# Staging fresh silus in the halves of the edge tile, inner residues first, and other places for the statistics' work and the silu stores

## The chip, the cores and the metric

One core of a Trainium2 chip runs the whole program. Its engines are TensorE (PE, with its weight loads as PEld), VectorE (DVE), ScalarE (ACT), GpSimd (POOL) and SyncE (SP), which here only issues DMA transfers, one after another in the program's order. The metric is the device time of one execution in microseconds (us); the time before is the median of three runs.

## The reference

The input is `x` of 4 x 128 x 96 x 96 in float32. A group norm (32 groups) is followed by a scan block that runs over four readings of each image (columns and rows, each forward and reversed), and the four results are fused by a 1x1 convolution and added to `x`. The block, for one reading:

```python
t = _grouped1x1(x, in_proj_w, in_proj_b, G)
u, gate = (t[:, :HID], t[:, HID:])
u = jax.nn.silu(u)
u = conv over 5 neighbours along the sequence, depthwise
s = _conv1x1(u, ssm_in_w)
a = DMIN + (DMAX - DMIN) * sigmoid(_conv1x1(u, ssm_delta_w, ssm_delta_b))
bb, cc = tanh(_conv1x1(u, ssm_b_w, ssm_b_b)), tanh(_conv1x1(u, ssm_c_w, ssm_c_b))
prefix = jnp.cumsum(jnp.log(a), axis=-1)
hst = jnp.exp(prefix) * jnp.cumsum(bb * s * jnp.exp(-prefix), axis=-1)
u = u + _conv1x1(cc * hst + ssm_d * s, ssm_out_w)
u = _grouped1x1(u * sigmoid(gate), mix_w, mix_b, G)
return _conv1x1(u, out_proj_w, out_proj_b)
```

There are 256 hidden channels and 32 states. The kernel folds the norm into the projection's weights, and the last two convolutions and the fusion into one matrix (`w_fin`).

## The kernel before

**Pairs, steps, phases.** A sequence of 9216 places is cut into 6 stretches of 16 image lines and 4 residues (place modulo 4), 384 places each. One *pair* handles one residue of one stretch for the forward and the reversed reading together. Four pairs, in the order of residues 1, 2, 3, 0, are a *step*; six steps are a *phase* (columns or rows of one image); eight phases, a column and a row phase for each of the four images (batches), make 48 steps and 192 pairs, numbered t = 0 to 191. So batches 2, 3 and 4 begin at steps 12, 24 and 36, that is with pairs 48, 96 and 144.

**Fresh and mirrored steps.** The reversed reading meets the same places from the other end. Therefore only the first three steps of a phase (the *fresh* ones) compute the projection and its Silu; the other three read them backwards: the fourth and fifth still have the tiles of the third and second, and the sixth loads what the first step stored. The gates (tanh halves of sigmoid) of the first half are kept in DRAM in the same way and loaded back (`load_kept`) two pairs before they are used, into two tiles that alternate.

**Fronts.** A front (`new_front`, `new_silu`, `new_stage`, `new_rest`) makes one residue of a later step: four matmuls, three Silus on ACT, and the moves. Channels 128 to 255 go straight to their plane of the step's `sil` tile. Channels 0 to 127 must lie in another order of partitions (32 channels times 4 residues), so ACT writes them to a *stage*, and four DMAs of 98.6 kB move it to `sil` (L525). There are two stages, cut from the tile `shared`; front g uses stage g modulo 2, so it has to wait until the moves of the front two before have landed. In pair t the front of residue index t + 5 is made, five pairs ahead of its step's first pair. During the warm-up (pairs 0 to 5) whole fronts are made five pairs ahead by simpler code, and the tenth is made in pair 6 in two halves that share two banks.

**The lone edge.** For residues 0 and 3 the five taps reach into a neighbouring column of which one residue alone is needed, in the plain order of channels. DVE adds it (`add_lone`, L766) from the tile `lone`, which holds the silus of residues 0 and 3 in stage order: 4 slots, two for residue 0 and two for residue 3. For that, each fresh step stores the two stages of residues 0 and 3 to DRAM (`edge`, or `front` for the first step), and `load_lone` (L757) loads both, 770 KB, at each step's first pair, except where the fourth step reuses the third's.

**One pair** (`pair_on`). PE: convolution into banks 6 and 7 (L130 on `band` and `less`), the output products of an older pair (L130 on `w_fin`), the z products (L649) mixed with a gate's or a front's matmuls (L629, L491), then the projection to the states (L130 `psum<-u,main`). DVE: four taps (L819), the edge (L766) in pairs of residues 3 and 0 (*short* pairs, whose convolution needs no `less`), a scan in the first two pairs of a step (L894), the gating of the pair six before (L710). ACT: copies, tanhs, the first tap of the next pair (L817), behind the gating, and then the front's stage (L518), which reads the banks that the next convolution writes. POOL: decay, products of the scan, and the additions into the accumulator. The order of all engines is written out by hand; nothing is rescheduled.

**Statistics.** While a column phase runs, the next image is loaded in 24 chunks (`xs`, L429), two for each short pair, and `bn_stats` (L437) runs on each. The rest (`stats_finish`: `bn_aggr`, small products, a square root by Newton steps on POOL, scaled weights, their rolled copy by DMA) is spread over pairs of the row phase by a table of places (pair within the phase, point in the pair).

**The start of a phase** also stores the first step's silus (`keep_silu`, L565, two stores of 770 KB), and in the column phases of later batches finished lines go out (L913) and new image lines come in (L1059).

## Time and profile before

| | us |
|---|---|
| median of three runs (lowest, highest) | 1758.65 (1758.1, 1760.34) |
| the profiled execution | 1758.79 |
| its span, from first to last instruction | 1757.0 |
| PE busy | 1713.8 |
| DVE busy | 1508.5 |
| ACT busy | 1484.5 |
| POOL busy | 1470.6 |
| step 1 (pairs 4 to 7, warm-up) | 36.27 |
| step 44, pairs 176 to 179 | 34.75 |
| step 12 (first of batch 2) | 42.80 |

A line of the profile names the source line, the engine, the operation and the tiles (out<-in), then how often and how long, and behind the bar or in brackets the idle time before it with what ended it. A wait that names ACT or DVE may be the end of a chain that a late DMA began. Matmul ends are modelled and overlap. The 16 DMA engines moved 386.30 MB, 220 GB/s over the span, but unevenly: between 123 and 307 GB/s in fortieths of the span. Rows of stretches give for each engine the busy time and, in brackets, the instructions; their ends were chosen at the starts of projections, so that a stretch is one step.

### The profile page before, as it was taken

Reading aid. Unit: us, or ns where it says so; the run is one execution under the profiler, and the core shown is the slowest. Engines: PE = TensorE matmul, PEld = TensorE weight load, DVE = VectorE, ACT = ScalarE, POOL = GpSimd, SP = SyncE. Lnnn points to the kernel's source line nnn. Section 1 sums busy time; section 2 is a strip of 40 time slices with the busy share of each in tenths; the row PEclk is TensorE's granted clock in tenths of the full one; section 3 lists DMA queues with packets and bytes.
Section 4 is the critical chain, followed back from the end, with each engine's and each line's share of the span. In section 5 each row is a group of like instructions: output and inputs, shape, how many; then the busy total and the mean of one; then the engine's idle time right before and its main releaser. Section 6 shows DMA issues by size and latency. Waiting matters only on the chain.

```text
span 1757.0 us, 50266 instructions
## 1 busy us (share of the span) xinstructions
PE 1713.8 (98%) x20410; PEld 705.5 (40%) x20410; DVE 1508.5 (86%) x1508; ACT 1484.5 (84%) x2438; POOL 1470.6 (84%) x1452
## 2 busy tenths in 40 slices
PE   7999999999999999999989999999999999999998
PEld 3343344344343434444434434444344443444333
DVE  6899999888789998888878999888887888888897
ACT  4788888888788888888968888888887888888875
POOL 3589898988678989888867898988787889998887
PEclk9999999999999999999999999999999999999999
DMA  7755896468995788547899487843899638873475
GB/s 240 224 181 181 268 260 194 139 208 243 296 307 187 227 245 242 176 134 253 246 294 296 147 251 240 250 155 133 246 276 298 232 123 273 238 212 131 134 238 175
DMA packets 149382, 386.30 MB, mean 220 GB/s; under 512 B 19873, under 2 KB 86305, under 8 KB 149153
## 3 DMA queue, kind: packets, MB, share of 16 engines
q1 hardware_dynamic: 149008, 383.05, 70.5%
q8 instruction: 162, 2.65, 0.6%
q14 instruction: 68, 0.55, 0.1%
q10 hardware_dynamic: 144, 0.04, 0.0%
HBM read 215.12 MB, written 133.01 MB: 198 GB/s over the span
## 4 chain that ended last, share of the span: by engine, by line
PE 86%; DMA 5%; DVE 2%; ACT 2%; POOL 2%; issue 1%; SPq 0%; ACTq 0%; POOLq 0%; DVEq 0%
PE psum L130 70%; PE psum L649 6%; PE psum L629 5%; PE psum L491 4%; DMA gate<-kept 2%; DMA kept<-shared 1%; DMA out<-acc 1%; ACT shared L518 1%; DVE t L894 1%; DMA sil<-shared 1%; DVE u L710 1%; DVE psum L819 1%; DMA acc<-in_xr 1%; POOL t L900 0%; POOL t L868 0%
## 5 line engine op out<-in xcount | busy, mean ns | idle before, releaser
L819 DVE SCALAR_TENSOR_TENSOR psum<-sil,small,psum 128x768 f32<-128x768 f32 x576 | 589.1, 1023 | 51.5 <-ACT psum L817 32.4
L130 PE MATMUL psum<-u,w_fin 128*32 128x384 f32 (+1 forms) x6192 | 558.9, 488 | 1.1 <-ACT ys L935 0.4
L130 PE MATMUL psum<-u,main 128*32 128x384 f32 x6144 | 535.6, 489 | 1.6 <-DVE u L1003 1.1
L710 DVE SCALAR_TENSOR_TENSOR u<-gate,psum 128x768 f32<-128x768 f32 x376 | 341.8, 950 | 150.9 <-PE psum L649 66.2
L954 POOL TENSOR_TENSOR acc<-ys,acc 128x384 f32<-128x384 f32 x375 | 442.0, 1202 | 12.5 <-ACT ys L935 1.9
L130 PEld LDWEIGHTS psum<-u,w_fin 128*32 128x32 f32 x6192 | 204.9, 110 | 310.3 <-issue 209.6
L661 ACT COPY psum<-u 128x768 f32<-128x768 f32 x384 | 306.8, 799 | 6.8 <-DVE u L710 4.0
L130 PEld LDWEIGHTS psum<-u,main 128*32 128x32 f32 x6144 | 180.1, 110 | 327.9 <-issue 207.0
L900 POOL TENSOR_TENSOR t<-t,t 64x384 f32<-64x384 f32 (+1 forms) x192 | 262.8, 1369 | 57.1 <-DVE t L894 37.4
L130 PE MATMUL psum<-sil,band 128*32 128x384 f32 x3072 | 290.1, 489 | 19.6 <-ACT shared L518 18.0
L867 POOL TENSOR_SCALAR t<-tm 64x384 f32<-64x384 f32 x188 | 179.6, 956 | 134.6 <-ACT tm L856 122.5
L649 PE MATMUL psum<-t,main 32*128 32x384 f32 x1536 | 272.8, 520 | 3.0 <-ACT psum L661 2.3
L901 POOL TENSOR_TENSOR t<-t,t 64x384 f32<-64x384 f32 (+1 forms) x192 | 236.9, 1234 | 15.1
L868 POOL TENSOR_TENSOR t<-t,tm 64x384 f32<-64x384 f32 x192 | 227.0, 1182 | 25.4 <-ACT t L859 10.3
L817 ACT ACTIVATE psum<-sil,small 128x768 f32<-128x768 f32 x191 | 172.0, 901 | 35.4 <-DVE u L710 31.5
L819 DVE SCALAR_TENSOR_TENSOR u<-sil,small,psum 128x768 f32<-128x768 f32 x192 | 194.9, 1015 | 6.8
L937 ACT COPY ys<-psum 128x384 f32<-128x384 f32 x288 | 138.4, 481 | 53.1 <-PE psum L130 42.6
L130 PEld LDWEIGHTS psum<-sil,band 128*32 128x32 f32 x3072 | 106.7, 109 | 170.8 <-issue 71.4
L629 PE MATMUL psum<-x_in,wn 32*128 32x384 f32 x768 | 162.4, 497 | 0.0
L491 PE MATMUL psum<-x_in,wn 32*128 32x385 f32 x704 | 149.7, 503 | 1.7 <-ACT shared L518 1.0
L503 ACT ACTIVATE sil<-psum,bnorm 128x385 f32<-128x385 f32 x176 | 102.4, 583 | 48.3 <-PE psum L491 35.4
L665 ACT ACTIVATE gate<-psum,bnorm 128x384 f32<-128x384 f32 x168 | 97.4, 582 | 43.4 <-PE psum L629 26.7
(110 smaller groups left out, 1701.0 us busy)
## 6 DMA issues: line engine op xcount, KB each, us to landing
gate<-kept SPq DMA_DIRECT2D x106, 768.0 KB, 5.7
kept<-gate SPq DMA_DIRECT2D x82, 768.0 KB, 3.8
sil<-shared SPq DMA_DIRECT2D x352, 96.2 KB, 3.5
sil<-sil SPq DMA_DIRECT2D x32, 770.0 KB, 8.2
lone<-edge SPq DMA_DIRECT2D x26, 770.0 KB, 8.6
x_in<-in_xs SPq DMA_DIRECT2D x194, 96.2 KB, 3.3
out<-acc SPq DMA_DIRECT2D x46, 384.0 KB, 7.5
x_in<-in_xs SPq DMA_DIRECT2D x88, 192.5 KB, 5.3
```

The source lines that it names most:

```text
L130: nc.tensor.matmul(o[r, : rhs.shape[-1]], lhsT, rhs, start=start, stop=stop, skip_group_check=True)
L491: nc.tensor.matmul(bank(banks[2 * j + s])[:, : N + 1], stats[units[step * UB]["b"]][0][a, s, :], x_in[s][a, q, :], start=True, stop=True,)
L629: nc.tensor.matmul(bank(to)[:, :N], stats[un["b"]][0][r, s, :], x_in[s][r, q, off : off + N], start=True, stop=True)
L649: nc.tensor.matmul(bank(ssm(bi, s) + j)[:, :N], w_so[r, bass.ts(j, P)], z[r, :], start=(bi, s) not in seeded, stop=True, skip_group_check= ...
L661: nc.scalar.copy(psum[:, ssm(bi, s) : ssm(bi, s) + 2, :N], us[bi][:, s])
L710: nc.vector.scalar_tensor_tensor(v, g, 1.0, pz, ALU.add, ALU.mult)
L819: nc.vector.scalar_tensor_tensor(us[i][:, :, 1, :] if k == K - 1 else part, src, w_tap[:, k : k + 1], part, ALU.mult, ALU.add,)
L867: nc.gpsimd.tensor_scalar(*decay(i))
L868: nc.gpsimd.tensor_mul(ta[0:64, p, :], tb[0:64, :], tm[0:64, :])
L900: engine.tensor_mul(ta[0:64, p, r], tb[64:P, r], ta[64:P, p, r])
L901: engine.tensor_add(tb[0:64, r], ta[0:64, p, r], tb[0:64, r])
L954: adder.tensor_add(part, y, part)
```

## The change

It does the following.

- Fronts take the residues in the order 1, 2, 0, 3 (`PLANES`) instead of 0, 1, 2, 3. The two loads of projection inputs per step take the planes 1 and 2, then 0 and 3 (`SETS`), and the saved planes of the first step are split in the same way: planes 1 and 2 are contiguous, 0 and 3 are not.
- A front's stage is a half of the step's own `lone` tile: front f uses half f modulo 2. After the fourth front the tile holds residues 0 and 3, in the order in which `add_lone` reads them. So fresh steps from step 2 on have no load of `lone`: 22 loads less. First and third steps of a phase use `shared` for it, second steps the tile that mirrored steps load into.
- Only second steps store edges to DRAM (and first steps their `front`); third steps no longer do.
- The two stores of a first step's silus are issued one pair earlier.
- Chunks of statistics begin in the phase's second step in batches 2 and 3, as they do in the first batch, and end in the next phase's first step. `stats_finish` keeps its operations, each two to five pairs later.
- In the warm-up, front 10 is made in pair 5 behind front 9.
- In pairs 55, 103 and 151 the decay runs on POOL again instead of ACT.

The core of the diff:

```diff
+PLANES = (1, 2, 0, 3)
+    SETS = (slice(1, 3), slice(0, R, 3))
...
-            (0, 0): gather,
-            (1, 1): means,
...
-            (3, 0): guess,
...
-            (8, 2): roll,
+            (6, 0): gather,
+            (7, 1): means,
...
+            (10, 0): guess,
...
+            (14, 2): roll,
...
-        places = singles * 2
-        if ph == 0:
-            places = (singles[2:] + [NP + 2, NP + 3]) * 2
+        places = (singles[2:] + [ph * NP + NP + 2, ph * NP + NP + 3]) * 2
...
+    def stage_of(step, f):
+        return lone[step][:, 2 * (f % 2) : 2 * (f % 2) + 2, :]
...
+        if st == 0:
+            nc.sync.dma_start(kept_front[e][PLANES[f]], stage)
+            if f == R - 1:
+                keep_silu(step, 0)
+        elif st == 1:
+            if f > 1:
+                nc.sync.dma_start(edge_of(step)[f - 2], stage)
+            if f == 0 and step > 1:
+                keep_silu(step - 1, 1)
...
+    def lone_tile(step):
+        if step % NS in (0, 2) and step > 1:
+            t = shared()[:, : 4 * (N + 1)]
+        else:
+            t = wk.tile([P, 4 * (N + 1)], F32, tag="lone", bufs=1, name=f"lone_{step}")
+        return t.rearrange("p (a n) -> p a n", n=N + 1)
...
-        by_scalar = i == NU - 2 or i > 2 * NP and i // 2 % (2 * NP) == 7
+        by_scalar = i == NU - 2
...
-            else:
-                whole_front(t + R, (4, 5, 2, 3) if banks != PROJ else (6, 7, 2, 3))
+            for f in {4: (8,), 5: (9, 10)}.get(t, ()):
+                whole_front(f, (4, 5, 2, 3) if banks != PROJ else (6, 7, 2, 3))
...
-        elif k == 0:
+        elif k == 0 and un["st"] > NS // 2:
             load_lone(un["step"])
...
-            later.update({(a + R, at): f for (a, at), f in stats_finish(un["b"] + 1).items()})
+            later.update(stats_finish(un["b"] + 1))
```

How it moves instructions, at three places. First, the queue of SP from the last front of step 12 on (pairs 46 to 48). `sil_202` is the saved silus in DRAM, `front_204` and `edge_1` are stored stages, `acc` and `out` are image lines in and out, `xs` chunks, `gate_` the tiles of kept gates. Before:

```order
L534 DMA front_204<-shared 128x770
L1059 DMA acc<-in_xr 128x2x384 x2
L913 DMA out<-acc 128x2x384 x2
L429 DMA xs_0_4665<-in_xr 128x384
L429 DMA xs_1_4667<-in_xr 128x384
L525 DMA sil_4690<-shared 32x770 x4
L686 DMA gate_177<-kept_6_196 128x1536
L536 DMA edge_1_207<-shared 128x770
L565 DMA sil_202<-sil_4305 128x1540
L757 DMA lone_4738<-front_204 128x2x770
L429 DMA xs_2_4758<-in_xr 128x384
L525 DMA sil_4690<-shared 32x770 x4
```

and next `L686 DMA gate_176<-kept_1_191`; the second store to `sil_202` comes behind that gate. Now, up to the same gate:

```order
L532 DMA front_204<-shared 128x770
L566 DMA sil_202<-sil_4295 128x1540
L1068 DMA acc<-in_xr 128x2x384 x2
L922 DMA out<-acc 128x2x384 x2
L523 DMA sil_4677<-lone_4678 32x770 x4
L687 DMA gate_177<-kept_6_196 128x1536
L566 DMA sil_202<-sil_4295 256x1x770
L523 DMA sil_4677<-lone_4678 32x770 x4
L687 DMA gate_176<-kept_1_191 128x1536
```

Both stores of saved silus stand ahead of the second gate; chunks, edge store and edge load are gone from this stretch.

Second, ACT in pairs 5 and 6 of the warm-up (L503 or L505 the Silus into `sil`, L518 or L516 the stage, L661 or L662 the copies ahead of the z products). Before:

```order
L503 ACTIVATE sil_743<-psum,bnorm_268 128x385 x2
L518 ACTIVATE shared<-psum,bnorm_268 128x770
L856 ACTIVATE tm_1_2_0_842<-psum,small 128x384
L859 COPY t_0_1_2_0_825<-psum 64x384
L865 ACTIVATE t_0_1_2_0_825<-psum,small 64x384
L661 COPY psum<-u_0_1_0_378 128x2x384
L503 ACTIVATE sil_743<-psum,bnorm_268 128x385 x2
L518 ACTIVATE shared<-psum,bnorm_268 128x770
L661 COPY psum<-u_0_1_0_378 128x2x384
```

Now:

```order
L505 ACTIVATE sil_743<-psum,bnorm_268 128x385 x2
L516 ACTIVATE shared<-psum,bnorm_268 128x770
L505 ACTIVATE sil_743<-psum,bnorm_268 128x385 x2
L516 ACTIVATE shared<-psum,bnorm_268 128x770
L865 ACTIVATE tm_1_2_0_852<-psum,small 128x384
L868 COPY t_0_1_2_0_835<-psum 64x384
L874 ACTIVATE t_0_1_2_0_835<-psum,small 64x384
L662 COPY psum<-u_0_1_0_378 128x2x384 x2
```

The tenth front's three Silus moved from between the two copies of pair 6 to ahead of pair 5's own tanhs.

Third, DVE in step 7, where `bn_aggr` (L236 or L237) ends the sums of batch 2 (L894 is the scan, L766 or L775 the edge). Before:

```order
L819 SCALAR_TENSOR_TENSOR u_1_1_0_2894<-sil_2460,small,psum 128x2x384
L894 SCALAR_TENSOR_TENSOR t_6_2594<-t_6_2594 64x768
L236 BN_AGGR mv_2474<-bn_868 128x2
L710 SCALAR_TENSOR_TENSOR u_5_3_0_2323<-gate_176,psum 128x768 x2
L819 SCALAR_TENSOR_TENSOR psum<-sil_2460,small,psum 128x2x384 x3
```

Now:

```order
L828 SCALAR_TENSOR_TENSOR u_1_3_0_3074<-sil_2457,small,psum 128x2x384
L775 SCALAR_TENSOR_TENSOR u_1_3_0_3074<-lone_2458,small,psum 128x2x384
L237 BN_AGGR mv_2472<-bn_878 128x2
L711 SCALAR_TENSOR_TENSOR u_0_1_0_2516<-gate_176,psum 128x768 x2
L828 SCALAR_TENSOR_TENSOR psum<-sil_2457,small,psum 128x2x384 x3
```

It moved from the step's first pair, behind a scan, to its third, behind the edge.

More of the change, by code (lines that the diff above doesn't have):

```diff
@@ L752, in keep_lone @@
                 )
+    def lone_tile(step):
[4 more added lines that the diff above has]
+        return t.rearrange("p (a n) -> p a n", n=N + 1)
     def load_lone(step):
[L755 to L757 removed]
+        lone[step] = lone_tile(step)
+        nc.sync.dma_start(
+            lone[step].rearrange("p (e s) n -> p e s n", e=2), edge_of(step).rearrange("e p s n -> p e s n")
+        )
     def add_lone(i, banks):
```

81 lines of the change are left out of this document (29 added, 52 removed).

## Prediction

> **What bounds the kernel now.** I read the page's busy shares and chain first, then the waits of TensorE (PE).
>
> ```profile
> PE 1713.8 (98%) x20410; PEld 705.5 (40%) x20410; DVE 1508.5 (86%) x1508; ACT 1484.5 (84%) x2438; POOL 1470.6 (84%) x1452
> ...
> PE 86%; DMA 5%; DVE 2%; ACT 2%; POOL 2%; issue 1%; SPq 0%; ACTq 0%; POOLq 0%; DVEq 0%
> ...
> PE psum L130 <- ACT shared L518: 18.0, 13, 4.5
> ```
>
> PE is busy for 98% of the span and makes 86% of the chain. Of its 43 us of idle time 18.0 lie before a convolution whose PSUM banks the stage's Silu (L518) still has to read. The change takes no matmul away, so it wins only where PE pauses or runs slowly. To find these places I cut the span at the starts of the projections, four pairs (one step) to a stretch. The rows are steps 6, 7, 12 (the second batch begins), 24 (the third), 36 (the fourth), 42 and 43; the last three numbers are the granted clock, the share of time that the 16 DMA engines are busy, and GB/s.
>
> ```profile
> 238.94:273.85 34.91, 34.91 (x417) 14.97 (x417) 32.29 (x33) 30.68 (x50) 31.80 (x29) 1.00 0.93 258
> 273.85:309.51 35.66, 35.21 (x432) 14.96 (x433) 31.14 (x34) 30.74 (x50) 31.78 (x37) 1.00 0.56 178
> 449.41:492.21 42.80, 37.33 (x418) 15.42 (x417) 31.27 (x33) 31.38 (x50) 28.80 (x29) 0.96 1.03 295
> 878.89:924.50 45.61, 38.58 (x417) 16.88 (x417) 31.40 (x33) 31.39 (x50) 31.46 (x32) 0.93 1.04 290
> 1311.46:1351.48 40.02, 37.28 (x417) 16.06 (x417) 29.50 (x29) 31.39 (x50) 30.52 (x30) 0.96 1.04 299
> 1526.83:1561.89 35.06, 35.06 (x417) 14.90 (x416) 30.54 (x29) 30.67 (x50) 31.92 (x29) 1.00 0.85 249
> 1561.89:1596.79 34.90, 34.89 (x417) 14.94 (x417) 29.15 (x29) 30.61 (x50) 31.70 (x29) 1.00 0.58 184
> ```
>
> An undisturbed step takes 34.9 to 35.1 us. Steps 12, 24 and 36 take 42.80, 45.61 and 40.02, and of these rows they alone have DMA engines busy all the time (1.03, 1.04, 1.04) and a clock below 1.00. Steps 6 and 42 do the same matmuls in 34.98 on average, so the three excesses are 7.82 + 10.63 + 5.04 = 23.5 us. What waits there, first by SP's queue, then VectorE (DVE), then PE; the last two rows are the fourth batch's wait and the busy stretch of the second:
>
> ```profile
> 448.93 0.33 SPq L686 DMA_DIRECT2D gate<-kept  x1
> ...
> 458.53 0.33 SPq L686 DMA_DIRECT2D gate<-kept  x1
> ...
> 473.29 0.34 SPq L686 DMA_DIRECT2D gate<-kept  x1
> ...
> 458.04 1.82 DVE L710 SCALAR_TENSOR_TENSOR u<-gate,psum 128x768 f32<-128x768 f32 x2 [0.73 <-PE psum L649]
> ...
> 469.62 1.82 DVE L710 SCALAR_TENSOR_TENSOR u<-gate,psum 128x768 f32<-128x768 f32 x2 [3.44 <-DMA gate<-kept]
> ...
> 482.11 0.56 DVE L437 BATCH_NORM_STATS2 bn<-xs 128x6 f32<-128x384 f32 x1 [4.97 <-DMA xs<-in_xr]
> ...
> 472.38 1.57 PE L130 MATMUL psum<-sil,band 128*32 128x384 f32 x16 [2.62 <-ACT shared L518]
> 473.70 4.45 PE L130 MATMUL psum<-u,w_fin 128*32 128x384 f32 x32
> ...
> 1340.15 1.82 DVE L710 SCALAR_TENSOR_TENSOR u<-gate,psum 128x768 f32<-128x768 f32 x2 [4.42 <-DMA gate<-kept]
> ...
> 440.00:501.40 61.40, 55.93 (x643) 22.69 (x640) 47.22 (x47) 47.81 (x76) 42.49 (x41) 0.97 1.03 299
> ```
>
> The queue is full. The gating (L710) of pair 50 waits 3.44 us for a kept gate; one pair later a chunk's statistics, ahead of the gating, wait 4.97 us for the chunk. ACT's first tap and its stage stand behind the gating, the stage empties the banks of the next convolution, and so 3.44 us of DVE become 2.62 of PE. The 32 products behind it then take 4.45 us. From 440 to 501 us the engines moved 299 GB/s at a share of 1.03: I take that as their capacity.
>
> The Trainium skill ("TensorE: Matmul & The Clock Gate", section "Why this matters for your kernels") puts the fall to half clock at idle gaps above about 3 us. Here a gap of 2.62 us was followed by slow products and the step's clock is 0.96, so the rows decide. By the page a gap this short would cost only itself, and the far end of A below would be 5 us nearer to the rest.
>
> **A: the queue at the three batch starts.** Kilobytes are from the page's list of issues.
>
> ```profile
> sil<-sil SPq DMA_DIRECT2D x32, 770.0 KB, 8.2
> lone<-edge SPq DMA_DIRECT2D x26, 770.0 KB, 8.6
> ...
> xs<-in_xr SPq DMA_DIRECT2D x72, 192.0 KB, 6.1
> ...
> edge<-shared SPq DMA_DIRECT2D x30, 385.0 KB, 6.5
> ```
>
> The late gate is the one issued at 458.53. Ahead of it in the busy stretch an edge store (385 KB; it moves behind), the edge load (770; gone) and three chunks (3 x 192; they begin a step later) go away, and the second store of saved silus (770, until now behind it) comes. Net 961 KB = 984 kB, at 299 GB/s 3.3 us earlier, against 3.44 us of lateness: 0.1 us is left. The next gate (issued 473.29) had both saves ahead of it already, so it gains 385 + 770 + 576 = 1731 KB, 5.9 us. Its landing has no row: not before 473.29 + 5.7 (the page's median for such loads) = 479.0, and not after 482.6, when its gating began without waiting for it. So 473.1 to 476.7 in the new order. It is needed one short pair after the gating of pair 50, for which DVE was free at 469.62 - 3.44 = 466.2. The length of a short pair is the distance of two projections (the last two rows):
>
> ```profile
> 427.15 2.76 PE L130 MATMUL psum<-u,w_fin 128*32 128x384 f32 x32
> ...
> 431.62 2.79 PE L130 MATMUL psum<-u,main 128*32 128x384 f32 x32
> ...
> 439.98 2.79 PE L130 MATMUL psum<-u,main 128*32 128x384 f32 x32
> ```
>
> That is 8.4 us, so it is needed at 474.6 and comes between 1.5 early and 2.1 late. PE sees about 0.8 less than DVE (3.44 against 2.62); I take 0.4 us of PE for pairs 50 and 51 together, near the middle. The chunk's wait cannot recur, since no chunk is left there; its work, moved to step 18, finds what step 6 has now, and step 6 takes 34.91 with it where step 42 takes 35.06 without. In the fourth batch there are no chunks; edge store and load are 1155 KB, 4.0 us of 4.42, and 0.8 swallows the rest.
>
> The store that is pulled forward can hurt. The first one now stands ahead of the gate issued at 448.93 in place of two chunks: 386 KB more, 1.3 us. An ordinary 5.7 us would put that gate at 454.6, and it was in time for 458.04: 0 to 1.3 us late, taken as 0, as the median lands 2 us clear. The slow products go with the pauses (4.45 - 2.76 = 1.7 us a time, within the steps' excess). So A = -23.5 + 2 x 0.4 = **-22.7**. Its far end: in each start 1.3 - 0.8 and 2.1 - 0.8 of pause and 1.7 of clock, 3.5 x 3 = 10.5, so -13.
>
> The skill ("DMA: Bandwidth & Descriptors", "Specifications") gives a core 358 GB/s of HBM, where 299 is what a full queue reached here. By 358 the 984 kB would be worth only 2.7 us, the gate would stay 0.7 late, and A would be about -22.
>
> **B: the statistics.** `bn_aggr` runs in the first pair of step 7, behind the scan and ahead of the gating:
>
> ```profile
> 273.65 0.81 DVE L236 BATCH_NORM_AGGREGATE mv<-bn 128x2 f32<-128x144 f32 x1
> ```
>
> Step 7 takes 35.66, its like without statistics (step 43) 34.90: 0.76. In the new order it stands in a short pair without scan or chunk. Two short pairs of step 6 carry two chunks' statistics each, and that step takes 34.91, so 0.81 should fit. GpSimd's small operations go two or three pairs later, to neighbours of the same kind. B = 3 x -0.7 = **-2.1**; ends -2.3 and 0.
>
> **C: the warm-up.** Front 10 moves from pair 6 into pair 5.
>
> ```profile
> 74.19 1.38 PE L491 MATMUL psum<-x_in,wn 32*128 32x385 f32 x4 [0.67 <-ACT sil L503]
> 76.57 0.91 PE L491 MATMUL psum<-x_in,wn 32*128 32x385 f32 x2 [1.00 <-ACT shared L518]
> ...
> 75.61 0.91 ACT L518 ACTIVATE shared<-psum,bnorm 128x770 f32<-128x770 f32 x1 [1.00 <-DMA sil<-shared]
> ```
>
> Its two hand-overs of banks cost PE 1.67 us in pair 6. But its stage reuses the half that front 8 filled, and waited for that half's transfers until 75.61. From pair 5 it waits for the same landing, with three small activations of pair 5 queued behind it on ACT, each shorter than its 0.91, and the next convolution waiting for its banks. Between -1.7 and +2.7; I take **0**.
>
> **D: the rest.** Three decays (0.96 us) go back from ACT to GpSimd (POOL), in pairs 55, 103 and 151, where POOL idles ahead of L868:
>
> ```profile
> 521.70 1.01 POOL L868 TENSOR_TENSOR t<-t,tm 64x384 f32<-64x384 f32 x1 [3.60 <-ACT t L859]
> ```
>
> So 0, and 2.9 without that cover. The other 19 edge loads, the edge stores of the third steps and the saves at four further phase starts lie in steps that PE fills (34.9 to 35.1): 0.
>
> **Sum.** -22.7 - 2.1 = -24.8. The profiled execution took 1758.79 (its span and 1.8 around it), 0.1 above the median 1758.65: I forecast **1734 us**.
>
> **Rivals.** *Half of it stays* (0.22). The busy stretch moved 299 x 61.4 us = 18.4 MB; the edge load, six chunks and an edge store are 2.4 MB of it, 13%. But without its pauses it is 8 us, also 13%, shorter, so the share stays near 1.0 and later gates may come late in turn, with the clock falling again. That is A's far end and B: 1758.8 - 13 - 2.1 = 1744, up to 1750 with a second such wait in each start.
>
> *No difference* (0.06). What makes the gate late is SP's turn or an order behind a stage, and not bytes; then B alone shows, 1756 to 1760. Against it: the share of 1.03, and issues of 0.33 us.
>
> *Slower* (0.06): the saves that are pulled forward. 770 KB enters ahead of a gate load at seven phase starts. If at all seven the gate then lands 3.4 us late or more (2.6 of pause after the 0.8, which is where the clock fell above), each pays 2.6 + 1.7 = 4.3 us, together 30, more than the 24.8: 1758.8 - 24.8 + 30 = 1764. Against it: at the second phase's start a gate is issued 13 us before it is needed.
>
> ```profile
> 234.62 0.53 SPq L686 DMA_DIRECT2D gate<-kept  x1
> ...
> 247.57 1.82 DVE L710 SCALAR_TENSOR_TENSOR u<-gate,psum 128x768 f32<-128x768 f32 x2 [0.96 <-ACT ys L937]
> ```
>
> **How the numbers follow.** Forecast 0.62 (its own range 1730 to 1739), more than that by C 0.04, half 0.22, none 0.06, slower 0.06. The range of 1729 to 1747 leaves out some 0.02 below and 0.17 above. Less than 0.2% (3.5 us) cannot be told from no change: faster 0.88, same 0.06, slower 0.06.
>
> **What would show it.** Right: steps 12, 24 and 36 at 35 to 36 us with a clock of 1.00, no wait of the gating on a kept gate above 1 us, DMA shares still near 1.0 there, step 7 at 34.9. Wrong: step 12 above 38 us, gatings of pairs 49, 51 or 53 waiting for gates with a slow clock beside them, or PE's pauses in pairs 5 and 6 more than 3 us above their present 1.67.

## The result and the profile after

The changed kernel takes **1736.46 us** (median of four, 1736.02 to 1738.14) where the kernel before takes 1759.49 beside it (1758.1 to 1760.96): a ratio of **0.9871**, 95% interval 0.9854 to 0.9888. The forecast was 1734 in a range of 1729 to 1747. The profiled execution took 1736.02 us, with a span of 1734.3 against 1757.0 before.

The page of the changed kernel, busy times and chain:

```profile
PE 1706.6 (98%) x20410; PEld 703.5 (41%) x20410; DVE 1506.4 (87%) x1508; ACT 1479.8 (85%) x2435; POOL 1478.3 (85%) x1455
...
PE 89%; DMA 4%; DVE 3%; ACT 2%; issue 1%; POOL 0%; SPq 0%; ACTq 0%; DVEq 0%; POOLq 0%
```

From the list of PE's waits, the convolution that waits for the stage's Silu (us in total, times, longest; before it was 18.0, 13, 4.5):

```profile
PE psum L131 <- ACT shared L516: 2.2, 6, 1.0
```

PE's idle time fell from 43.2 us (1757.0 - 1713.8) to 27.7 (1734.3 - 1706.6). The other 7 us of the gain lie in its busy time, which fell though it does the same matmuls: most of that is the clock, whose mean went from 0.995 to 0.998 (0.3% of the span, 5 us). The places are seen in the stretches from projection to projection. Steps 1, 6, 7, 12, 24, 25, 28 and 36 of the changed kernel; the last three numbers are granted clock, share of the DMA engines, GB/s:

```profile
61.10:98.40 37.30, 34.40 (x356) 13.79 (x352) 32.02 (x33) 27.22 (x44) 23.65 (x22) 0.91 0.64 184
239.10:274.32 35.22, 35.21 (x416) 15.06 (x417) 32.55 (x33) 30.65 (x50) 32.26 (x29) 1.00 0.83 234
274.32:309.52 35.20, 35.20 (x433) 15.22 (x435) 29.88 (x31) 30.62 (x50) 32.51 (x33) 1.00 0.37 109
449.15:484.37 35.22, 35.22 (x418) 15.02 (x417) 29.56 (x29) 31.38 (x50) 29.01 (x29) 1.00 1.04 313
869.90:905.11 35.21, 35.21 (x417) 14.99 (x416) 29.56 (x29) 31.38 (x50) 28.89 (x29) 1.00 1.03 306
905.11:941.42 36.31, 35.33 (x418) 14.84 (x417) 31.67 (x33) 30.97 (x50) 28.77 (x29) 1.00 0.88 271
1010.96:1048.34 37.38, 35.41 (x416) 13.56 (x416) 32.69 (x32) 30.78 (x51) 31.34 (x30) 1.00 0.89 271
1293.76:1328.97 35.21, 35.21 (x418) 15.01 (x417) 29.56 (x29) 31.37 (x50) 28.94 (x29) 1.00 1.05 312
```

The three batch starts went from 42.80, 45.61 and 40.02 us to 35.22, 35.21 and 35.21: 22.8 us, nearly the whole gain. PE is busy throughout, the clock is 1.00, and the DMA engines are as full as before (1.03 to 1.05). Two things were not forecast: step 1 is 1.0 longer than before (36.27), and steps 25 and 28 are longer too (35.38 and 35.98 before). Step 7 fell from 35.66 to 35.20, but step 6 rose from 34.91 to 35.22.

What the gatings of pairs 50, 51 and 52 now wait for, by the timeline of DVE:

```profile
466.24 1.82 DVE L711 SCALAR_TENSOR_TENSOR u<-gate,psum 128x768 f32<-128x768 f32 x2 [1.25 <-ACT ys L944]
...
474.61 1.82 DVE L711 SCALAR_TENSOR_TENSOR u<-gate,psum 128x768 f32<-128x768 f32 x2 [1.19 <-PE psum L650]
...
483.85 1.82 DVE L711 SCALAR_TENSOR_TENSOR u<-gate,psum 128x768 f32<-128x768 f32 x2 [1.21 <-ACT ys L944]
```

No gate stands late here. The loads for pairs 50 and 51 are issued at 455.24 and 465.57 and take 7.8 and 7.1 us to land, by SP's timeline and by the view of the tile `gate` at each of the two:

```profile
455.24 0.53 SPq L687 DMA_DIRECT2D gate<-kept  x1
...
465.57 0.34 SPq L687 DMA_DIRECT2D gate<-kept  x1
```
```profile
DMA to landing us min/median/max: 7.8/7.8/7.8
...
DMA to landing us min/median/max: 7.1/7.1/7.1
```

So they are there at 463.0 and 472.7, 3.2 and 1.9 us before their use. Measured from the start of the step, the gate for pair 50 lands 6.3 us earlier than before, when its gating began with it (469.62 - 449.41 against 463.0 - 449.15). About half of that is the landing, which took 11.0 us from the issue at 458.53 and now takes 7.8. The other 3.0 us are an earlier issue: 9.1 us into the step before (458.53 - 449.41), 6.1 now (455.24 - 449.15). The prediction's sum of bytes gave 3.3 in all. The total was right, but this term was not; the experiments follow it.

### The profile page after: what moved, and what is told of

It is laid out like the page before. It is cut to its first block, busy times and chain, and to the rows that moved or that the text cites. A ratio compares the mean times of both kernels' runs of the same rounds, so it can differ in the third digit from the quotient of the medians.

```text
span 1734.3 us, 50199 instructions
## 1 busy us (share of the span) xinstructions
PE 1706.6 (98%) x20410; PEld 703.5 (41%) x20410; DVE 1506.4 (87%) x1508; ACT 1479.8 (85%) x2435; POOL 1478.3 (85%) x1455
## 4 chain that ended last, share of the span: by engine, by line
PE 89%; DMA 4%; DVE 3%; ACT 2%; issue 1%; POOL 0%; SPq 0%; ACTq 0%; DVEq 0%; POOLq 0%
PE psum L131 72%; PE psum L650 6%; PE psum L630 5%; PE psum L492 5%; DMA kept<-shared 2%; DVE psum L828 1%; DMA sil<-shared 1%; DMA sil<-sil 1%; DVE t L903 1%; DVE u L711 1%; ACT psum L826 1%; DMA acc<-in_xr 0%; PE psum L1274 0%; ACT psum L662 0%; ACT shared L516 0%
## 5 line engine op out<-in xcount | busy, mean ns | idle before, releaser
L662 ACT COPY psum<-u 128x768 f32<-128x768 f32 x384 | 306.2, 798 | 7.1 <-DVE u L711 4.3
L877 POOL TENSOR_TENSOR t<-t,tm 64x384 f32<-64x384 f32 x192 | 235.6, 1227 | 15.3
L505 ACT ACTIVATE sil<-psum,bnorm 128x385 f32<-128x385 f32 x176 | 102.4, 583 | 48.7 <-PE psum L492 35.5
```

Of the source, the lines that this page charges most:

```text
L662: nc.scalar.copy(psum[:, ssm(bi, s) : ssm(bi, s) + 2, :N], us[bi][:, s])
L877: nc.gpsimd.tensor_mul(ta[0:64, p, :], tb[0:64, :], tm[0:64, :])
```

## The experiments

The table gathers the runs that bear on the batch starts, in us: the time between the projections of pairs 50 and 51 and of pairs 51 and 52, where the two delays of step 12 showed, the three steps, and the median of the runs. Where nothing is late, the two stretches take 8.36 and 9.29.

| kernel | 50 to 51 | 51 to 52 | step 12 | step 24 | step 36 | median |
|---|---|---|---|---|---|---|
| before | 12.72 | 12.51 | 42.80 | 45.61 | 40.02 | 1759 |
| before, chunks a step later | 8.36 | 13.79 | 39.72 | 40.85 | 41.82 | 1752.74 |
| before, no fresh edge loads | 8.36 | 11.67 | 37.60 | 37.44 | 35.22 | 1742.41 |
| before, edge loads of 24.6 KB | 8.36 | 13.64 | 39.57 | 40.84 | 35.21 | 1744.59 |
| before, chunks later, no edge loads | 8.36 | 9.29 | 35.21 | 36.60 | 35.22 | 1734.55 |
| before, saves earlier | 11.63 | 14.19 | 44.00 | 45.31 | 40.62 | 1761.66 |
| change, chunks at the old place | 8.36 | 14.47 | 40.41 | 40.81 | 35.22 | 1742.55 |
| change, edge load back | 9.43 | 9.95 | 36.95 | 37.59 | 37.83 | 1742.81 |
| change, six loads of 25 KB | 8.36 | 10.72 | 36.65 | 36.34 | 37.39 | 1741.12 |
| change | 8.36 | 9.29 | 35.22 | 35.21 | 35.21 | 1736.46 |

The steps are from one trace each, and one trace of such a start is good to about 2 us: the first edit does not touch step 36, which took 41.82 in its trace and 40.02 in the other.

**Chunks a step later, alone.**

```diff
-        places = singles * 2
-        if ph == 0:
-            places = (singles[2:] + [NP + 2, NP + 3]) * 2
+        places = (singles[2:] + [ph * NP + NP + 2, ph * NP + NP + 3]) * 2
```

> The kernel before with one edit: the chunks of batches 3 and 4 begin in the phase's second step, as in the change (nothing else of the change). Step 36 has no chunks in either kernel. Theory of bytes (the gate is late by the bytes ahead of it, at 299 GB/s): 3 x 192 KB fewer ahead of the late gates is 2.0 us. The first late gating waits 3.44 - 2.0 = 1.4 us instead of 3.44, the 4.97 us for the chunk are gone, the gate behind it comes up to 4 us late in its place: step 12 from 42.80 to 37 to 41, step 24 from 45.61 to 39 to 43, step 36 stays at 40.0, the whole -4 to -13 us, 1746 to 1755. Theory that the chunk's place is the main cause (its statistics stand ahead of the gating, and all else follows from that stall): steps 12 and 24 go to 36 or less, step 36 stays at 40.0, the whole about -16 us, 1743.

Ratio 0.9963 (0.9943 to 0.9984): 6.5 us, within the range of the theory of bytes; the chunk's place is not the main cause. But the gating of pair 50 waits for nothing now, where the sum left it 1.4 us late, and that of pair 51 waits 4.12. The DVE timeline of this kernel, then of the one without edge loads, then of the change with old chunks:

```profile
477.40 0.95 DVE L708 SCALAR_TENSOR_TENSOR u<-gate,psum 128x768 f32<-128x768 f32 x1 [4.12 <-DMA gate<-kept]
```
```profile
476.37 0.56 DVE L437 BATCH_NORM_STATS2 bn<-xs 128x6 f32<-128x384 f32 x1 [2.77 <-DMA xs<-in_xr]
```
```profile
475.61 0.56 DVE L438 BATCH_NORM_STATS2 bn<-xs 128x6 f32<-128x384 f32 x1 [3.81 <-DMA xs<-in_xr]
```

**No edge loads in fresh steps, alone.**

```diff
-        if k == 0 and un["st"] == NS // 2:
+        if k == 0 and un["st"] <= NS // 2:
             lone[un["step"]] = lone[un["step"] - 1]
```

> The kernel before without the edge loads of the fresh steps from step 2 on (those steps add the edge from the tile of an earlier step, so this part of the computation is not the reference's); edge stores, chunks and all else as before. Theory of bytes: 770 KB less is 2.6 us. Step 36 (4.42 us of lateness, no chunks) keeps 1.8 us, of which PE sees 1.0: 36.0. In steps 12 and 24 the gating keeps 0.8, the chunk 2.3, the next gate up to 5: 37 to 40 each, the whole -10 to -17, 1742 to 1749. Theory that the queue is not limited by bytes (the loads are late for another reason, such as a place in the order): steps 12, 24 and 36 stay above 39, the whole -3 to 0. The nineteen edge loads in other steps: 0 by both.

Ratio 0.9902 (0.9881 to 0.9923): 17 us. This is the larger part. The fourth batch's start is cured by it alone. In steps 12 and 24 pair 50 is cured, and pair 51 waits 2.77 us for its second chunk (the second row above).

**Saves one pair earlier, alone.**

```diff
             nc.sync.dma_start(kept_front[step // NS % 2][g], stage)
+            if g == R - 1:
+                keep_silu(step, 0)
...
-        if st == 1 and step > 1 and g < 2:
-            keep_silu(step - 1, g)
+        if st == 1 and step > 1 and g == 0:
+            keep_silu(step - 1, 1)
```

> The kernel before with one edit: the two stores of a first step's saved silus are issued one pair earlier, as in the change. Theory of bytes: 770 KB more stand ahead of the gate that is late by 3.44 us (4.42 in step 36), so it is late by up to 6 (7); the gates behind it have the same bytes ahead as before. Steps 12, 24 and 36 each gain 0 to 2.6 us, other phase starts nothing: the whole 0 to +8, my value +4, 1763. Rival of the prediction (slower): all seven phase starts pay a pause and slow products, 4.3 us each: +20 to +30. If neither is seen (below +1), stores do not stand in the loads' way as bytes.

Ratio 1.0010 (0.9997 to 1.0023): a loss of up to 4 us that the runs hardly resolve. The three starts changed by +1.2, -0.3 and +0.6, no more than traces differ. The clearest loss is at the second phase's start, step 6, which goes from 34.91 to 37.45 us; steps 18 and 30 went up by 1.0 and 0.4. So the mechanism of the rival "slower" exists, at 0.4 to 2.5 us at three of the phase starts and not at 4.3 at seven.

**The change with chunks at the old place.** The first edit, reversed.

> The changed kernel with one part undone: the chunks of batches 3 and 4 begin with the phase again. In the changed kernel the gate for pair 50 landed 1.9 us before its gating and that for pair 49 3.2 us before. Theory of bytes: three chunks ahead of them are 2.0 us, so the gate comes just in time or 0.1 late, and each chunk's own landing is in time: steps 12 and 24 at 35.2 to 36.5, the whole 0 to +2.5 against the changed kernel, 1736 to 1739. Theory that the chunk's place is the main cause: steps 12 and 24 above 39 again, the whole +8 or more. Step 36 stays at 35.2 by both.

(This expectation, and that of the edge load put back, number the gates one pair too low: the landings 3.2, 1.9 and 5.7 us early are those for pairs 50, 51 and 52.) Steps 12 and 24 are above 40 again: +10.8 us in the trace (the medians of the runs differ by 6.1), and the theory of bytes falls for the chunk. In the third row above the second chunk of pair 51 is late by 3.81. Its turn tells why. Only three chunk tiles exist, so it can be loaded when the first chunk of pair 50 has been read. These are that reading and SP's issues behind it, in this kernel:

```profile
462.82 1.01 DVE L438 BATCH_NORM_STATS2 bn<-xs 128x6 f32<-128x384 f32 x2
```
```profile
463.52 2.25 SPq L525 DMA_DIRECT2D sil<-lone  x3
466.11 0.34 SPq L689 DMA_DIRECT2D gate<-kept  x1
467.09 0.34 SPq L539 DMA_DIRECT2D edge<-lone  x1
468.13 0.33 SPq L430 DMA_DIRECT2D xs<-in_xr  x1
```

The tile is free at 463.4. SP comes to the load at 468.13, behind moves, a gate and an edge store, and the chunk's use ends its wait at 475.6, 12.2 us after the tile came free; a pair later it is needed. The chunk is late by SP's order and by the landing together, and no sum of bytes ahead of it shows that.

**Both edits in the kernel before.** The table so far reads as if pair 50 needed either edit and pair 51 both.

> The kernel before with two edits together: chunks that begin a step later, and no edge loads in fresh steps from step 2 on (their edge comes from an older step's tile, so this part of the computation is left out). Alone they left pair 51 waiting, the first for a gate (steps 12, 24, 36: 39.72, 40.85, 41.82), the second for a chunk (37.60, 37.44, 35.22). Theory now: pair 50 needs either, pair 51 needs both, because the later of two waits sets it. So steps 12, 24 and 36 come to 35.2 to 35.6, the whole 1734 to 1738, though the parts alone add up to more (7.8 and 18.2 against 23). Rival, that the change's edge stores and saves are needed as well: one of the three steps above 36.5, the whole above 1739.

Ratio 0.9864 (0.9846 to 0.9881), the change's own. Steps 12 and 36 are at 35.2, the least that any trace shows for them; in step 24 one gate came 2.7 us late. The two parts alone gave 7.8 and 18.2 us at the three starts (the first by steps 12 and 24), together 26, and both at once 21.4 in this trace: the waits of one pair are not added, the later of gate and chunk sets it. In pair 50 of step 12 either part alone takes the whole 4.4 us. In pair 51 the later chunks alone lose 1.3 us and the missing load alone gains 0.8, but both together gain 3.2. With the edge stores and the saves left as they were, these two edits give all of A but the 1.4 us of step 24.

**The edge load cut to 24.6 KB, in the kernel before.** Its turn on SP stays, its bytes nearly vanish:

```diff
-        if k == 0 and un["st"] == NS // 2:
+        if k == 0 and un["st"] <= NS // 2:
             lone[un["step"]] = lone[un["step"] - 1]
+            if un["st"] < NS // 2:
+                nc.sync.dma_start(lone[un["step"]][0:16, 0, :], edge_of(un["step"])[0, 0:16, 0, :])
```

> The kernel before, with each fresh step's edge load (from step 2 on) cut from 788 kB to 24.6 kB: the same turn on SP, hardly any bytes (those steps add the edge from an older step's tile, so this part of the computation is left out). Without the load altogether steps 12, 24 and 36 took 37.60, 37.44 and 35.22, the whole 1742.4. Theory of bytes: the same within 0.5 us each, 1741 to 1744. Theory of turns (a place in flight costs by itself, as six small loads did: 4.7 us over the three steps, 0.3 for each load and step): +0.3 each by that price, up to +2 each if a single turn is what tips the gate: 1742 to 1748. If it goes back to 40 or more in each, bytes play no part.

Step 36 needs only the bytes to go. Steps 12 and 24 give back 2.0 and 3.4 us of what the missing load had won (in one trace each; the medians, 1744.59 and 1742.41, have ranges that overlap). The chunk's wait grew from 2.61 to 4.38 us in step 24, but in step 12 only from 2.77 to 3.05. The rest of step 12 is the clock. Windows of 3.41 us around PE's pause, without the load (first two rows) and with the small one:

```profile
477.82:481.23 3.41, 1.63 (x19) 1.54 (x23) 3.23 (x4) 3.36 (x6) 1.04 (x2) 1.00 1.04 302
481.23:484.64 3.41, 3.41 (x50) 1.30 (x41) 3.34 (x3) 2.99 (x5) 3.41 (x3) 1.00 1.06 372
```
```profile
477.36:480.77 3.41, 1.12 (x17) 0.67 (x13) 3.27 (x5) 2.47 (x4) 0.19 (x1) 1.00 1.00 277
480.77:484.18 3.41, 3.41 (x28) 2.67 (x21) 3.31 (x4) 1.97 (x4) 3.33 (x4) 0.50 1.04 360
```

With PE busy for 1.63 us of its window the clock stays at 1.00; with 1.12 the next window is granted 0.50, and has 28 matmuls of PE in place of 50. So 0.3 us of lateness became 2.

**Bytes or turns, in the changed kernel.** The one load of 770 KB is put back, or six small ones in its place:

```diff
+        elif k == 0 and un["st"] == 0 and un["step"]:
+            nc.sync.dma_start(
+                lone[un["step"]].rearrange("p (e s) n -> p e s n", e=2),
+                edge_of(un["step"]).rearrange("e p s n -> p e s n"),
+            )
```
```diff
+        elif k == 0 and un["st"] == 0 and un["step"]:
+            for e in range(6):
+                r = slice(16 * e, 16 * e + 16)
+                nc.sync.dma_start(lone[un["step"]][r, 0, :], edge_of(un["step"])[0, r, 0, :])
```

> The changed kernel with one part undone: at the seven phase starts from the second on, the first step's edge (770 KB) is loaded again from DRAM at its old place, into the tile that holds it already. In the changed kernel the gates for pairs 49, 50 and 51 landed 3.2, 1.9 and 5.7 us before their gatings. Theory of bytes alone: 770 KB are 2.6 us, so the gate of pair 50 is 0.7 us late, which PE does not see: steps 12, 24 and 36 at 35.2 to 36, the whole 0 to +3 against the changed kernel, 1736 to 1740. Theory of turns (in all traces so far SP begins a transfer only when the one eight before it has landed, and a load that must follow its own store holds up what stands behind it on SP): the gate loads begin late, as in the kernel before with later chunks, whose step 12 took 39.7, step 24 40.9 and step 36 41.8: +3 to +6 for each of the three, 1746 to 1754. Other phase starts: 0 to +0.5 by both.

> As the kernel with the edge load put back, but in its place six loads of 25 KB each (16 partitions of the first slot), which carry 0.15 MB in place of 0.79: the same wait for the stores, more turns, few bytes. Theory of bytes: 148 KB are 0.5 us, within the 1.9 us to spare: steps 12, 24 and 36 at 35.2 to 35.4, the whole 0 to +0.5. Theory of turns: six places of the eight in flight are taken by small transfers and the gate behind them begins later: +1 to +5 for each of the three steps, the whole +3 to +15.

The large load costs 1.7, 2.4 and 2.6 us at the three starts, between the two theories. The six small ones, a fifth of its bytes, cost 1.4, 1.1 and 2.2: bytes alone fall, and a fixed price per turn falls too. (A half clock before the first projection, which no edit touches, is 7 us of the large load's profiled span.) In the kernel with six, SP's timeline, and SP's waits in that stretch:

```profile
448.22 0.58 SPq L687 DMA_DIRECT2D gate<-kept  x1
450.15 0.58 SPq L566 DMA_DIRECT2D sil<-sil  x1
451.11 3.41 SPq L1068 DMA_DIRECT2D shared<-front  x6
455.83 4.51 SPq L523 DMA_DIRECT2D sil<-lone  x4
460.44 0.53 SPq L687 DMA_DIRECT2D gate<-kept  x1
```
```profile
SPq L523 <- DMA sil<-sil: 2.2, 1, 2.2
...
SPq L523 <- DMA gate<-kept: 1.2, 1, 1.2
```

The first move waits for the landing of the gate at 448.22, the second for that of the save at 450.15, though a move needs neither. Each is the transfer eight before it. With the places taken by small transfers SP stands until the save has landed, and the gate for pair 50 is issued at 460.44 where the changed kernel has 455.24. Meanwhile the engines run short of work. Two equal stretches from step 12's start, with the six small loads and then in the changed kernel:

```profile
449.45:458.55 9.10, 9.10 (x113) 3.44 (x112) 8.14 (x8) 8.21 (x13) 7.03 (x8) 1.00 0.89 269
458.55:467.13 8.58, 8.58 (x101) 3.72 (x104) 6.94 (x8) 7.48 (x12) 8.04 (x9) 1.00 0.79 206
```
```profile
449.15:458.25 9.10, 9.10 (x113) 3.44 (x112) 8.18 (x8) 8.21 (x13) 7.03 (x8) 1.00 1.05 312
458.25:466.83 8.58, 8.58 (x102) 3.71 (x104) 6.95 (x8) 7.47 (x12) 8.04 (x9) 1.00 1.04 302
```

The engines fall to a share of 0.79 and 206 GB/s, so what was to move then moves later. The gate for pair 50 still lands in time, 4.9 us behind its issue. The gate for pair 51 is issued at 468.95 where the changed kernel has 465.57, and lands 6.4 us later, at 475.4. That is when its gating begins, 0.5 us later in the step than in the changed kernel:

```profile
475.45 1.82 DVE L711 SCALAR_TENSOR_TENSOR u<-gate,psum 128x768 f32<-128x768 f32 x2 [1.74 <-PE psum L492]
```

How these 0.5 us become the 1.4 that pair 51 is longer was not traced further.

**The statistics at their old places, in the changed kernel.**

```diff
-            (6, 0): gather,
+            (0, 0): gather,
...
-            later.update(stats_finish(un["b"] + 1))
+            later.update({(a + R, at): f for (a, at), f in stats_finish(un["b"] + 1).items()})
```

> The changed kernel with the statistics' later work back at its old places (two to five pairs earlier, the aggregation between a scan and a gating). The prediction's theory: steps 7, 19 and 31 go from 35.20, 35.01 and 35.01 to 35.7, steps 6, 18 and 30 stay at 35.22: the whole +2. Rival: the 0.3 us by which steps 6, 18 and 30 are longer than in the kernel before (34.9) come from the same move, so they fall back to 34.9 as steps 7, 19 and 31 rise: the whole +1 or less.

Neither. Steps 7, 19 and 31 go to 35.31, 35.32 and 35.31, 0.7 us in all, and steps 6, 18 and 30 stay at 35.22. The next run but one bears on what holds these up.

**The changed kernel again**, with no edit.

> The changed kernel once more, with nothing edited, beside these. Its first profile had three steps that I had not expected: step 1 at 37.30 (before 36.27), step 25 at 36.30 (35.38) and step 28 at 37.38 (35.98), together +3.4 us. Theory that they belong to the change: all three recur within 0.2 us. Rival, that they are chance of the full queue and of when the clock falls: they differ by more than 0.5 us, in either direction, and step 1 lies somewhere from 36.3 to 37.3, as it does in four looks at the kernel before's warm-up (36.26 to 36.98).

Median 1734.22 (1731.0 to 1741.63). Steps 25 and 28 came out at 35.07 and 35.79: their stalls were chance. Step 1 took 37.87, more than 0.2 us from the 37.30 of the first trace and above the range that chance was given, so neither sentence holds for it.

**Warm-up and saves undone.**

```diff
-            if f == R - 1:
-                keep_silu(step, 0)
...
-            if f == 0 and step > 1:
-                keep_silu(step - 1, 1)
+            if f < 2 and step > 1:
+                keep_silu(step - 1, f)
...
-            for f in {4: (8,), 5: (9, 10)}.get(t, ()):
-                whole_front(f, (4, 5, 2, 3) if banks != PROJ else (6, 7, 2, 3))
+            else:
+                whole_front(t + R, (4, 5, 2, 3) if banks != PROJ else (6, 7, 2, 3))
...
+        if n == 0:
+            i0, to = t + R, (4, 5, 4, 5)
...
+            new_rest(i0)
```

> The changed kernel with two parts undone that touch different steps: front 10 is made in pair 6 again, and the two stores of saved silus are issued one pair later again. Warm-up: in six looks at the changed warm-up step 1 took 36.37 to 37.87 (mean 37.4), in four at the old one 36.26 to 36.98 (mean 36.4). Theory that the change's warm-up costs: step 1 at 36.3 to 37.0, -0.9. Rival, chance: above 37.3. Saves: theory that pulling them forward costs only where a gate or a chunk is late anyway: steps 12, 24 and 36 stay at 35.2, steps 6, 18 and 30 at 35.2, 0. Rival, that it was part of the gain: one of the steps 12, 24, 36 above 36. The whole 1733 to 1736 by the first theories: at or a little below the changed kernel.

Median 1735.22 (1733.77 to 1739.74), ratio 0.9871 (0.9850 to 0.9892), not to be told from the change. By steps, with step 1, 6 and 7 in these rows:

```profile
68.47:104.73 36.26, 33.50 (x356) 13.73 (x352) 32.02 (x33) 27.15 (x44) 23.34 (x22) 0.95 0.65 189
245.70:280.60 34.90, 34.89 (x416) 14.91 (x416) 32.29 (x33) 30.64 (x50) 31.83 (x29) 1.00 0.81 247
280.60:315.80 35.20, 35.20 (x432) 15.16 (x434) 30.15 (x31) 30.68 (x50) 32.75 (x33) 1.00 0.37 109
```

Steps 6, 18 and 30 are back at 34.90: in the changed kernel the saves pulled forward cost 0.3 us in each, not 0. Steps 12, 24 and 36 stay at 35.2, so the saves were no part of the gain either. Step 1 is at 36.26 here; the next run has the same warm-up and 37.23.

**A store four turns earlier.** If turns count, a transfer can be helped without a byte less:

```diff
+        if gated is not None and gated % NP < 2:
+            nc.sync.dma_start(keep(gated)[:, :, 0], both)
         if gated is not None:
             for s in range(2):
                 load_gate(2 * gated + s + UB)
...
-        if gated is not None:
-            if gated % NP > 1:
-                nc.sync.dma_start(keep(gated), to)
-            else:
-                nc.sync.dma_start(keep(gated)[:, :, 0], both)
+        if gated is not None and gated % NP > 1:
+            nc.sync.dma_start(keep(gated), to)
```

> The changed kernel with the old warm-up and the later saves (as in the run before), and one edit more, in the pairs that make a later phase's first two gates (places 17 and 18 of a phase): the store of the larger half of these gates, until now issued behind two or four small loads of projection inputs, is issued ahead of them. No byte more or less. Steps 4, 16, 28 and 40 hold these pairs; without the edit they took 36.01, 36.04, 36.02 and 35.07, since in pairs 18 and 19 of the phase an activation waits until the store of an older half has landed. Theory of turns: two to four turns earlier are 0.6 us each or more, so the pairs 18 and 19 shorten from 8.9 to 9.3 and 9.3 to 9.7 us toward 8.4 and 9.2: steps 4, 16 and 28 at 35.2 to 35.7, together -1 to -2.4 us; the whole about 1733 (1731 to 1736), not to be told from the changed kernel by its time alone. Theory of bytes alone: the same bytes are ahead within 0.2 MB (0.7 us), so -0.3 or less for each step.

The stretch behind the phase's pair 18 fell from 8.94, 8.99, 9.29 and 8.56 us to 8.26 in all four phases. Steps 16 and 28 took 35.18 and 35.42 instead of 36.04 and 36.02, step 40 34.86 instead of 35.07, but step 4 35.97, as the next stretch took 10.28 there. The four sum to -1.7 us. Step 10, which holds the same pairs in a row phase, took 36.26 in this trace, and 34.88 to 35.34 in the seven others of the changed kernel and its variants; steps 22 and 34 did not move. So the wait aimed at is gone, and what the four turns gain as a whole is not settled by the trace. The median is **1732.88** (1732.06 to 1733.7), ratio 0.9848 (0.9830 to 0.9866), the lowest of all kernels run; its interval overlaps the change's.

## Why the prediction was right, and where it was not

**A, -22.7 forecast, -22.8 measured.** That the queue at the batch starts, through a late gate and a late chunk, held PE back, and that the edge load and the chunks were what filled it, is shown by the two edits alone and together. The products' slow clock went with the pauses, as forecast: the three starts had four windows of 3.41 us at half clock before and have none now. Two of the falls came behind pauses of 2.62 and 2.74 us, in steps 12 and 36, where the rule of 3 us from the Trainium skill ("TensorE: Matmul & The Clock Gate", section "Why this matters for your kernels") would have left the clock at 1.00. In the rows of the small edge load it falls after a window in which PE still had 1.12 us of work. The size is right partly by luck. The step "net 961 KB, 3.3 us earlier" undercounted: 6.3 us were measured, so the lateness that it left for PE (0.4 us in each of two starts, 0.8 in all) did not come. In its place 0.7 us are left for another reason: the three steps do not go below 35.2 in any trace, where the sum took 34.98 for an undisturbed step. That the saves cost 0 there held in the changed kernel. What was missing is that SP's place in the line moves with the number of transfers and with what the eighth before it is, so that the gate is also issued 3.0 us earlier.

**B, -2.1 forecast.** In the run with warm-up and saves undone, where the statistics' move stands beside the old saves, it takes steps 6 and 7 together from 70.57 to 70.10, 18 and 19 from 70.55 to 69.91, and 30 and 31 from 70.69 to 69.91, all against the kernel before: -1.9, right in size, though step 7 is at 35.20 and not at the 34.9 that was to show it. (That run differs from the kernel before in more; that the move does it is read from the place.) With the saves in place the move is worth only 0.7; why is not shown. The saves give back 0.3 in each of steps 6, 18 and 30, 0.95 in all. The prediction had them at 0 (under D), since PE fills these steps. PE is still busy throughout, and yet the last pair of each (27 in step 6) is 0.3 us longer. What lengthens it stays open, and it is not the saves alone: with the edge load put back these steps took 34.95, 34.90 and 34.90 though the saves are early.

**C, 0 forecast, about +0.8 measured, not clear of chance.** Six traces of the changed warm-up give step 1 as 36.37 to 37.87 (mean 37.4), eight of the old one 36.26 to 37.27 (mean 36.6). The price was in the range, and the pauses are as forecast: PE waits 2.18 + 0.72 us now where it waited 1.11 + 0.67 + 1.00. But three short ones have become a long and a short one, and what the clock makes of that was not costed. PE in windows of 3.41 us, changed kernel:

```profile
65.51:68.92 3.41, 1.33 (x24) 0.31 (x8) 3.34 (x5) 1.44 (x3) 1.75 (x2) 0.99 0.97 265
68.92:72.33 3.41, 3.30 (x12) 1.21 (x16) 3.33 (x3) 2.20 (x5) 1.97 (x2) 0.50 1.01 284
72.33:75.75 3.42, 3.42 (x28) 1.02 (x24) 2.04 (x2) 1.08 (x2) 0.90 (x2) 0.51 0.80 230
```

The pause leaves PE 1.33 us of one window, and two windows at half clock follow. Where the same pause fell across two windows (step 1 at 36.37, in the change with old chunks) one half window followed. The number of such windows sorts all fourteen traces: step 1 takes 36.26 to 36.37 us with one window at half clock and 36.98 to 37.87 with two. Two came in five of six traces of the changed warm-up and in three of eight of the old one. A split as uneven as this comes by chance in about one case of eight, so it is not shown that the changed warm-up costs anything.

**D, 0 forecast.** Steps 13, 25 and 37, where the decay returned to POOL, went from 35.62, 35.38 and 35.43 to 35.07, 35.07 and 35.08 (the changed kernel again): -1.2 us. In the kernel before with both edits, which keeps ACT's decays, they are at 35.41, 35.35 and 35.41, so ACT's shorter turn may be what gains there; it was not run alone. The other steps without edge loads stayed as they were, within 0.3 us, as forecast.

**The sum.** Of the 22.7 us between the two profiled spans, 22.8 are A, 0.9 B with the saves, -1.0 C, 0.9 steps 13 and 37, -2.3 the chance stalls of steps 25 and 28, 0.6 the time to the first projection, and 0.8 small changes elsewhere.

**The rivals.** "Half stays" did not come: the share of the engines stayed at 1.03 to 1.05, as that rival argued, but no gate was late. That the share is full, then, does not say that a load is late: it has to be read where the load lands. "No difference" (SP's turn and not bytes) was given 0.06 because issues took only 0.33 us; half of its argument was true, for SP's turn does count, but the change shortens the turns as well. "Slower" lives on at some phase starts: 0.3 us in the changed kernel, 0.4 to 2.5 in the kernel before with the saves alone.

## What to carry to other kernels

Where a load is late, look at what its issue waited for as well as at the bytes ahead; here that was the landing of the transfer eight before it. Dropping a transfer was worth more than its bytes here, and issuing a store before small loads that nobody waits for took a wait away without a byte less. Where one pair has two waits, cost the later of them and not their sum: an edit that cures one alone can be worth little, and both together much, as in pair 51. A pause of PE is best kept below half of a clock window, going by the windows counted below.

## What the runs showed of the hardware

- **Eight transfers of SP in flight, by the program's own semaphores.** In all fourteen traces no transfer of SP is issued before the one eight places earlier has landed, as far as landings are recorded (smallest distance 0.015 us); in the kernel before, 192 of 1225 issues come within 0.3 us after it. 270 issues come ahead of the landing of the seventh before, and none within 0.3 us after that of the ninth before. In the kernel before, the gate at 458.53 stands eight behind the edge store at 449.95. SP's timeline, the landing of that store, and what the gate's issue waited for:

```profile
449.95 0.33 SPq L536 DMA_DIRECT2D edge<-shared  x1
450.99 0.32 SPq L565 DMA_DIRECT2D sil<-sil  x1
452.02 0.37 SPq L757 DMA_DIRECT2D lone<-front  x1
452.70 1.03 SPq L429 DMA_DIRECT2D xs<-in_xr  x1
453.83 2.69 SPq L525 DMA_DIRECT2D sil<-shared  x4
458.53 0.33 SPq L686 DMA_DIRECT2D gate<-kept  x1
```
```profile
DMA to landing us min/median/max: 8.5/8.5/8.5
```
```profile
SPq L686 <- DMA edge<-shared: 1.9, 1, 1.9
```

  449.95 + 8.5 is 458.45. Where the number eight comes from stands in the traces' records of SP's instructions. In all fourteen, SP's transfers tell of their landing by eight semaphores (counters that an instruction can wait for), taken in turn. For 1191 of the 1225 issues in the kernel before, SP itself waits for the transfer's own semaphore first, which the eighth before it used: the gate at 458.53 and the edge store at 449.95 share one. So these are waits of the program. How many transfers the chip would take without them, no run tells.

- **The clock goes by windows, and one that is 61% idle was enough.** Behind the warm-up, in all traces, the 14 windows of 3.41 us in which PE ran at full clock and was busy for 0.39 of the time or less were each followed by a window at half clock, and of 22 with 0.46 to 0.75 none was. In the warm-up the bound lies higher: some windows with 0.59 to 0.80 were followed by a fall, others not. The Trainium skill ("TensorE: Matmul & The Clock Gate", section "What's actually happening") also has free-running windows of about 3.4 us, which the traces bear out; it speaks of an idle window, and here one idle gap of 2.08 us inside a window sufficed (the kernel before with saves earlier, at 916.73 us).

- **Full queues moved different amounts at the same share.** The three batch starts of the changed kernel reach 306 to 313 GB/s at a share of 1.03 to 1.05. Ahead of the first projection, where the first image comes in, the changed kernel's queue reaches 356:

```profile
10.00:20.00 10.00, 8.01 (x25) 4.85 (x26) 8.94 (x18) 0.00 (x0) 1.13 (x4) 1.00 1.03 356
```

  So the 358 GB/s of the Trainium skill ("DMA: Bandwidth & Descriptors", "Specifications") is reached there within 1%, and is not the price of a byte over a batch start, though single windows of 3.41 us reach 360 and 372 there (the rows of the edge load cut to 24.6 KB). Which of the transfers make the difference is not shown.

- **A half clock of 13.7 us before the first projection** in three of fourteen profiles (the changed kernel again, the edge load put back, and the run with warm-up and saves undone) put that projection 7 us later, at 42.2 to 42.5 instead of 33.8 to 36.1. The windows ahead of it had PE busy for 0.84 to 0.87. The changed kernel has it in one of its two profiles and not in the other, so it is chance there, and one reason why single executions of the changed kernel range from 1731.0 to 1741.63.
